# Slots declared in three dimensions, and a new order of the steps at the ends of the layers, in a fused RWKV kernel

## The chip, the cores and the metric

The kernel runs on one core of one Trainium2 chip. The metric is the device time of one execution in microseconds (us), lower is better. The kernel before was run three times: 5460.03, 5460.32 and 5466.32 us, median 5460.32.

## What is computed

The input x is (16, 192, 56, 56) float32: 16 images, 192 channels, T = 3136 positions. Three RWKV layers with different weights follow one another, then one graph convolution. Each adds its result to x:

```
for each of 3 layers:
    n = group_norm(x)                     # 32 groups of 6 channels, over all T positions
    k, v, r = Wk n, Wv n, Wr n            # 192 x 192 products at each position
    f = scan over t = 0..T-1              # decay w per channel, bonus u on the current position:
        y_t = (p + e^(u+k_t) v_t) / (q + e^(u+k_t)),   p = e^w p + e^k_t v_t,   q = e^w q + e^k_t
    b = the same scan over t = T-1..0
    h = sigmoid(r) * (f + b) / 2
    x = x + Wo (layer_norm over channels of h)
last: n = group_norm(x)
      x = x + gelu(batch_norm(conv_w [n, max of n's four neighbours at distance 2, minus n, at least 0]))
```

The group norm needs the sums over all positions of an image before the next layer can begin. That is what makes a layer have an end.

## The kernel before

All the time is spent in `fast_path`. Two images form a pair, and a tile of one pair is 128 partitions x 3 rows x columns: row 0 is 128 channels of the first image, row 2 those of the second, and row 1 the last 64 channels of both. The positions are cut into 7 chunks of L = 448 columns.

**Slots.** Chunks of x, e^k (`ek`), e^k v (`ekv`), the scans' results (`q`, `p`; `den` and `h` for the forward pass) and the sigmoid (`sg`) live in 33 slots of SBUF, which are handed out and given back in a queue (class `Slot`, L501). A slot is declared as one flat stretch of 3 * (L + 2) + 2 floats a partition. The three rows are views of it: `t` is the 448 data columns of each row, `full` has one more column at the right, `lead` one more at the left. The extra column carries two things. A scan (`scan`, L834) reads the last state of the chunk before it there, put there by `save` (L850), so that a scan of 449 columns continues it. And in the first chunk of a product it carries the mean of the group norm (`mean_column`, L753), so that PE computes the bias of a projection as one more column, which `take_bias` (L825) copies out. The semaphores between engines are placed by the framework from the regions that the instructions read and write.

**Order of the work.** Pairs run in two streams. While one stream runs its backward pass over chunks 6 to 0, the other runs its forward pass, so that a step in the middle has a backward chunk and a forward chunk (`both_a`, L1244, or `both_c`, L1336, beside the convolution). Each pass has seven chunks, shifted by one: the last forward chunk (6) is a step by itself (`forward_a`, L1386), then the first backward chunk (6) is one (`backward_alone`, L1505), then come the six double steps, of which the first is `both_a_first` (L1295) when the partner is a forward pass. The order inside a step is written out by hand: every engine takes its instructions in the order of the calls. A forward pass begins 24 times (8 pairs, 3 layers), and the convolution 8 times.

**A backward chunk** goes through: `b_gate` (product r on PE), `b_exp` (e^-r on ACT), `b_sigmoid`, `b_q`, `b_p` (scans on DVE), `b_den`, `b_num` (bonus on `ek` and `ekv`, two instructions at L860 each), inversion of `ek` on ACT (`ln` L923, `exp_minus` L926), `b_mix` (nine products on POOL, L986 to L988), `b_squares` (ACT), `b_sums` (PE), `b_rs1` (ACT, L1010), `b_rs2` (DVE, L1014), `b_rs3` (ACT, L1019 and L1020), `b_spread` (PE, L1026), `b_scale` (DVE, L1031), `b_out` (PE, the product with Wo), `b_x` (DVE, L1044) and the store, then `b_stats` (sums and squares for the next group norm, ACT, L725 and L726). `late` keeps how far a chunk has come.

**A forward chunk**: `a_values` (product v on PE; in the last chunk also `mean_column`, for r's bias), `a_q`, `a_save`, `a_den`, `a_ekv` (L898), `a_p`, `a_num`, `a_y` (POOL, L930), and `a_keys`, `a_exp` for the next chunk.

**A layer's end.** After chunk 0's `b_x`, `b_stats` runs the check of the finished layer's bounds (`require_all`, L632: one comparison at L634, one minimum at L635) and calls `begin_later` (L781), which loads the next weights and puts three parts in a list: `norm_sums` (DVE reduces the statistics at L731, PE sums the groups), `norm_var` (small DVE instructions from L738 on, `mean_column`, two on ACT) and `norm_fold` (three small DVE products and a scaling, L764 to L767; then the weights of k and v are scaled on DVE and those of r on POOL, three instructions each at L757 to L759). Each `gap()` in a step's order runs the next part of the list. `keys` runs what is left, so that `run.begun` is set before the first product of k.

Of the kernel before, what the change touches and what calls it, by code (L numbers as in the profile page):

```python
# [34 lines left out]
F32 = mybir.dt.float32  # L35
# [4 lines left out]
P = 128  # L40
# [14 lines left out]
L = 448  # L55
# [418 lines left out]
def fast_path(ctx: ExitStack, tc: tile.TileContext, flag, x, wproj, wfold, wcfold, wconst, wgroup, sums, picks, vecs, out):  # L474
# [19 lines left out]
    def name(s):  # L494
        ngen[0] += 1
        return f"{s}_{ngen[0]}"
# [4 lines left out]
    class Slot:  # L501
        def __init__(self, what):
            self.tag = free.pop(0)
            flat = keep.tile([P, 3 * (L + 2) + 2], F32, tag=self.tag, name=name(what))
            rows = lambda at: flat[:, at : at + 3 * (L + 2)].rearrange("p (j n) -> p j n", j=3)[:, :, 0 : L + 1]
            self.full, self.lead = rows(2), rows(1)
            self.t = self.full[:, :, 0:L]

        def give(self):
            free.append(self.tag)  # L510
# [14 lines left out]
    def stile(s, n=1):  # L525
        return small.tile([P, 3, n], F32, tag=s, name=name(s))
# [113 lines left out]
    def layer_params(l):  # L640
        b = NPAR * l
        dec = decays[:, 2 * l : 2 * l + 2]
        cc = const.tile([P, 2], F32, tag=f"cc{l}", name=f"fcc{l}")

        edge = const.tile([P, 3, 1], F32, tag=f"edge{l}", name=f"fedge{l}")
        grow = const.tile([P, 3, 1], F32, tag=f"grow{l}", name=f"fgrow{l}")
        w = small.tile([P, 2], F32, tag="p2", name=name("w"))
        S.activation(w, vec[:, b + DECAY_, :], AF.Exp)
        S.activation(dec, w, AF.Exp, scale=-1.0)
        for j in range(3):  # L650
            S.activation(edge[:, j, :], w[:, column(j)], AF.Exp, scale=-float(T))
            S.activation(grow[:, j, :], w[:, column(j)], AF.Exp, scale=float(T))
        G.tensor_scalar(edge, edge, -1.0, None, ALU.mult)
        uw = small.tile([P, 2], F32, tag="p2", name=name("uw"))
        V.tensor_sub(uw, vec[:, b + U_, :], w)
        require(slice(0, 2), uw, UW_MIN, ALU.is_ge)
        require(slice(0, 2), uw, UW_MAX, ALU.is_le)
        S.activation(cc, uw, AF.Exp)
        V.tensor_scalar(cc, cc, -1.0, None, ALU.add)

        wo = wos[l]
        bt = stile("lnb")
        for j in range(3):
            V.tensor_copy(bt[:, j, :], vec[:, b + BETA_, column(j)])
        ps = banks("pswob")
        project(ps, packed(wo), of(bt), 1)
        wob = const.tile([P, 2], F32, tag=f"wob{l}", name=f"fwob{l}")
        V.tensor_copy(wob[:, 0:1], ps[0][:, 0:1])
        V.tensor_copy(wob[:, 1:2], ps[1][:, 0:1])
        release(*ps)  # L670

        V.tensor_scalar(wo[:, 0:C], wo[:, 0:C], vec[:, b + GAMMA_, 0:1], None, ALU.mult)
        V.tensor_scalar(wo[:, C:WCOLS], wo[:, C:WCOLS], vec[:, b + GAMMA_, 1:2], None, ALU.mult)
        rest = cslot.t[:, 1 + l % 2, 0:C]
        V.tensor_copy(rest[:, 0:P], wo[:, C : C + P])
        V.tensor_copy(rest[LO, P:C], wo[LO, C + P : C + P + 64])
        V.tensor_copy(rest[HI, P:C], wo[HI, C + P + 64 : WCOLS])
        ps = banks("psctr")
        project(ps, packed(cmat), lambda rows, j: rest[rows, :] if j == 1 else wo[rows, 0:C], C)
        V.tensor_copy(wo[:, 0:C], ps[0][:, 0:C])  # L680
        V.tensor_copy(wo[:, C : C + P], ps[1][:, 0:P])
        V.tensor_copy(wo[LO, C + P : C + P + 64], ps[1][LO, P:C])
        V.tensor_copy(wo[HI, C + P + 64 : WCOLS], ps[1][HI, P:C])
        release(*ps)
        return dec, cc, edge, grow, wob, packed(wo)
# [21 lines left out]
    class Run:  # L707
        def __init__(self, pr, l, stats, src=None, first=None):
            self.pr, self.l, self.stats, self.src = pr, l, stats, src
            self.xa, self.xb, self.xz = {}, {}, {}  # L710
            if first is not None:
                self.xa[0] = first
            self.begun = False
            self.bias, self.ps = {}, {}
            self.ek, self.ekv, self.h, self.den, self.sg, self.rs = {}, {}, {}, {}, {}, {}
            self.m, self.ml, self.q, self.p = {}, {}, {}, {}
# [12 lines left out]
    def norm_sums(run):  # L729
        mv = small.tile([P, 2, 3], F32, tag="mv", name=name("mv"))  # L730
        V.tensor_reduce(mv, run.stats, mybir.AxisListType.X, ALU.add)  # L731
        run.ps["g"] = bank("psg")
        project_small(run.ps["g"], full_rows(gmat), lambda rows, j: mv[rows, :, j], 2)

    def norm_var(run):
        m = run.ps["g"][:, 0:6].rearrange("p (j s) -> p j s", s=2)
# [24 lines left out]
    def norm_fold(run):  # L761
        rstd, t = run.rstd, stile("gt")

        V.tensor_mul(t, rstd, rstd)  # L764
        V.tensor_mul(t, t, run.var)
        V.tensor_scalar(t, t, -0.5, 1.5, ALU.mult, ALU.add)
        V.tensor_mul(rstd, rstd, t)  # L767
        w, wr = run.weights
        if run.l == NLAYERS:
            V.tensor_sub(w[:, 0, :], w[:, 0, :], w[:, 1, :])  # L770
        fold(V, w, rstd)
        run.w = [folded(w[:, 0, :]), folded(w[:, 1, :])]
        if run.l < NLAYERS:
            fold(G, wr, rstd)
            run.w.append(folded(wr[:, 0, :]))
            run.new = new_stats()
        run.begun = True

    norms = []

    def begin_later(run):  # L781

        kv = wpool.tile([P, 2, FCOLS], F32, tag="kv", name=name("wkv"))
        if run.l == NLAYERS:
            nc.sync.dma_start(kv, wcfold)
            run.weights = kv, None
        else:
            nc.sync.dma_start(kv, wfold[run.l, :, 0:2, :])
            r = wpool.tile([P, 1, FCOLS], F32, tag="r", name=name("wr"))
            nc.sync.dma_start(r, wfold[run.l, :, 2:3, :])  # L790
            run.weights = kv, r
        load_ahead(("C" if run.l == NLAYERS else "A", run, 0))
        norms.extend((part, run) for part in (norm_sums, norm_var, norm_fold))

    def gap():
        if norms:
# [107 lines left out]
    def a_save(run, c):  # L904
        if c < NL - 1:
            save(run.den[c], AHEAD, slot_of(run.ek, c + 1, "ek"), S)
        else:
            run.last = stile("cq")
            S.activation(run.last, run.den[c].t[:, :, L - 1 : L], AF.Copy)

    def a_p(run, c, eng=G):
# [28 lines left out]

    def b_gate(run, c):
        product(run, "r", run.w[2], run.xb[c], c == NL - 1)
        if c == NL - 1:
            take_bias(run, "r", S, -1.0)

    def b_exp(run, c):
        ps, b = run.ps["r"], run.bias["r"]
        sg = run.sg[c] = Slot("sg")
        for j in ORDER:
            at = j * NL + c  # L950
            S.activation(  # L951
                sg.t[:, j, :], ps[j][:, 0:L], AF.Exp, bias=b[:, j, :], scale=-1.0, accum_out=run.chk[:, at : at + 1]
            )
            release(ps[j])
# [96 lines left out]
    def b_stats(run, c):  # L1051
        xs = run.xb.pop(c)
        chunk_stats(run.new, xs.t, c, c == 0)
        if c == 0:
            require_all(run.chk, slice(0, NCHK))
            nxt = run.follow
            nxt.stats, nxt.src = run.new, run.dst
            nxt.xa[0] = xs
            begin_later(nxt)
        else:  # L1060
            xs.give()
# [81 lines left out]
    for pr in range(npairs):  # L1143
        runs = [Run(pr, 0, new_stats() if pr < 2 else None)]
        for l in range(NLAYERS):
            runs[-1].follow = Run(pr, l + 1, None)
            runs[-1].dst = [dram.tile([P, 3, L], F32, tag=f"x{pr}_{l}_{c}", name=name("xd")) for c in range(NL)]
            runs.append(runs[-1].follow)
        chains.append(runs)
# [63 lines left out]
    def deviation(u):  # L1213
        b_rs1(*u)
        b_rs2(*u)
        b_rs3(*u)
        late[u] = 1
# [77 lines left out]
    def both_a_first(b, a, nback, nfront):  # L1295
# [16 lines left out]
        b_squares(*l, (1,))  # L1312
        if nback is not None:
            b_gate(*nback[1:])
            b_exp(*nback[1:])
        b_sums(*l)
        deviation(l)
        a_q(*a)
        keys(nfront)
        spread_and_scale(l)  # L1320
        b_squares(*b, (0,))
        a_save(*a)
        exp_keys(nfront)
        b_squares(*b, (2, 1))
        b_sums(*b)
        a_p(*a, V)
        a_den(*a)
        b_rs1(*b)
        ln(den())
# [56 lines left out]
    def forward_a(a, nback, nfront):  # L1386
# [19 lines left out]
        if l:  # L1406
# [16 lines left out]
            a_num(*a)  # L1423
            add(l)
            sum_up()
        else:
            if ahead:
                exp_keys(nfront)
# [76 lines left out]
    def backward_alone(b, nback, nfront):  # L1505
# [4 lines left out]
        b_q(*b)  # L1510
        gap()
        b_den(*b)
        gap()
        invert(b[0].ek[b[1]])
        b_sigmoid(*b)
        b_p(*b)
        gap()
        b_num(*b)
        b_mix(*b)
        for u in list(late):  # L1520
            finish(u)
        if nback is not None:
# [56 lines left out]
        assert not late and not unsummed  # L1579


    least = small.tile([P, 1], F32, tag="least", name="fleast")
    V.tensor_reduce(least, ok, mybir.AxisListType.X, ALU.min)
    ps = bank("psok")

# [92 lines left out]
```

## Time and profile before

The profiled execution took 5459.15 us, of which its span, from the first to the last instruction, is 5457.3 us.

| what | value |
|---|---|
| median of three runs | 5460.32 us |
| profiled execution, span | 5459.15 us, 5457.3 us |
| mean granted TensorE clock | 0.908 |
| DVE scans (L845) | 2016, 1070 ns each |
| DVE bonus (L860), 128x896 and 128x448 | 1151 to 1382 ns and 686 to 922 ns |
| POOL products: L986 to L988, L930 | about 1.2 us and 3.04 us each |
| POOL scaling of r's weights (L757 to L759) | 24 x (1.04 + 0.92 + 1.39) us |
| ACT's wait before the bias copies of r (L830) | 113.9 us in all |

A row of a timeline has the start in us from the span's start, the duration in us, the engine, the line of the code, the operation, the tile written and those read, the form (partitions x columns), and how many instructions are merged in it; in brackets stands the idle time of the engine ahead of it and what ended it. A row of a list of waits has the waiting engine, tile and line, then what it waited for, with the total in us, the count and the longest.

### The profile page before, as it was taken

Reading aid. Unit: us, or ns where it says so; the run is one execution under the profiler, and the core shown is the slowest. Engines: PE = TensorE matmul, PEld = TensorE weight load, DVE = VectorE, ACT = ScalarE, POOL = GpSimd, SP = SyncE. Lnnn points to the kernel's source line nnn. Section 1 sums busy time; section 2 is a strip of 40 time slices with the busy share of each in tenths; the row PEclk is TensorE's granted clock in tenths of the full one; section 3 lists DMA queues with packets and bytes.
Section 4 is the critical chain, followed back from the end, with each engine's and each line's share of the span. In section 5 each row is a group of like instructions: output and inputs, shape, how many; then the busy total and the mean of one; then the engine's idle time right before and its main releaser. Section 6 shows DMA issues by size and latency. Waiting matters only on the chain. (4 is left out here: it accounts for less than half of the span.)

```text
span 5457.3 us, 51046 instructions
## 1 busy us (share of the span) xinstructions
PE 4665.8 (85%) x15206; PEld 1502.5 (28%) x15206; DVE 5028.0 (92%) x6628; ACT 3640.3 (67%) x6891; POOL 2769.3 (51%) x2164
## 2 busy tenths in 40 slices
PE   6888988989798898888879888888888888898897
PEld 2222322223222222222222222222222222222222
DVE  6889999999999999999999999999989999999996
ACT  6776766766676676676666766666667566676673
POOL 1555555645454465554454455555535455555453
PEclk8889988989899898898989989988898999998898
DMA  5222212224343211213424212221343312122233
GB/s 147 76 78 71 83 65 75 69 92 130 95 130 88 81 66 68 73 67 110 144 76 146 66 63 76 73 73 61 114 133 92 108 56 73 61 83 78 76 101 112
DMA packets 314272, 482.43 MB, mean 88 GB/s; under 512 B 66432, under 2 KB 306688, under 8 KB 313984
## 3 DMA queue, kind: packets, MB, share of 16 engines
q1 hardware_dynamic: 312832, 477.59, 27.6%
q8 instruction: 123, 2.02, 0.2%
q10 hardware_dynamic: 1152, 1.48, 0.1%
q14 instruction: 165, 1.35, 0.1%
HBM read 324.83 MB, written 154.14 MB: 88 GB/s over the span
## 5 line engine op out<-in xcount | busy, mean ns | idle before, releaser
L845 DVE TENSOR_TENSOR_SCAN q<-fdecays,ek 128x449 f32<-128x449 f32 (+1 forms) x1008 | 1024.6, 1071 | 23.8 <-POOL p L930 13.7
L845 DVE TENSOR_TENSOR_SCAN p<-fdecays,ekv 128x449 f32<-128x449 f32 (+1 forms) x1008 | 1023.6, 1070 | 4.3 <-POOL p L930 1.6
L986 POOL TENSOR_TENSOR ekv<-ekv,ek 128x448 f32<-128x448 f32 x504 | 620.3, 1231 | 707.9 <-ACT ek L926 354.5
L930 POOL TENSOR_TENSOR p<-p,q 128x1344 f32<-128x1344 f32 x168 | 510.2, 3037 | 884.2 <-ACT q L926 469.9
L987 POOL TENSOR_TENSOR p<-p,ekv 128x448 f32<-128x448 f32 x504 | 607.5, 1205 | 39.5
L988 POOL TENSOR_TENSOR p<-p,sg 128x448 f32<-128x448 f32 x504 | 600.8, 1192 | 51.7 <-ACT ek L854 8.0
L856 POOL COPY ekv<-p 128x3 f32<-128x3 f32 x271 | 188.3, 695 | 734.8 <-DVE p L845 385.7
L1026 PE MATMUL rsb<-rs,fpicks 32*128 32x448 f32 (+1 forms) x1008 | 370.7, 649 | 166.8 <-ACT rs L1020 166.8
L880 ACT ACTIVATE ek<-k,k 128x448 f32<-128x448 f32 x504 | 293.9, 634 | 287.9 <-PE k L596 261.6
L995 ACT ACTIVATE ek<-p 128x448 f32<-128x448 f32 x504 | 283.8, 573 | 266.1 <-POOL p L988 264.6
L593 PE MATMUL ops<-p,fwo 128*128 128x448 f32 x336 | 230.5, 777 | 229.7 <-DVE p L1031 229.0
L860 DVE SCALAR_TENSOR_TENSOR q<-ek,fcc,q 128x896 f32<-128x896 f32 x336 | 348.6, 1038 | 60.4 <-ACT ek L854 52.0
L726 ACT ACTIVATE fjunk<-x 128x448 f32<-128x448 f32 x672 | 387.5, 577 | 20.4
L860 DVE SCALAR_TENSOR_TENSOR ek<-ek,fcc,q 128x896 f32<-128x896 f32 x336 | 367.2, 1093 | 8.7 <-POOL chk L936 2.8
L725 ACT ACTIVATE fjunk<-x 128x448 f32<-128x448 f32 x600 | 343.1, 572 | 12.9
L860 DVE SCALAR_TENSOR_TENSOR ekv<-ekv,fcc,p 128x896 f32<-128x896 f32 x336 | 340.7, 1014 | 7.3
L1044 DVE SCALAR_TENSOR_TENSOR x<-ops,fwob,x 128x448 f32<-128x448 f32 x504 | 314.7, 673 | 27.0 <-PE ops L602 19.6
L860 DVE SCALAR_TENSOR_TENSOR p<-ekv,fcc,p 128x896 f32<-128x896 f32 x336 | 308.6, 919 | 20.4 <-POOL ekv L856 13.6
L951 ACT ACTIVATE sg<-r,r 128x448 f32<-128x448 f32 x504 | 312.2, 625 | 19.0 <-PE r L596 13.4
L898 DVE SCALAR_TENSOR_TENSOR ekv<-v,v,ek 128x448 f32<-128x448 f32 x504 | 312.8, 676 | 0.6
L1031 DVE TENSOR_TENSOR p<-p,rsb 128x448 f32<-128x448 f32 x504 | 282.7, 614 | 31.4 <-PE rsb L1026 31.2
L923 ACT ACTIVATE ek<-ek 128x1344 f32<-128x1344 f32 x168 | 221.1, 1316 | 71.6 <-DVE ek L860 71.6
(232 smaller groups left out, 11540.2 us busy)
## 6 DMA issues: line engine op xcount, KB each, us to landing
x<-xd SPq DMA_DIRECT2D x240, 672.0 KB, 5.6
xd<-x SPq DMA_DIRECT2D x168, 672.0 KB, 3.9
x<-in_x_dram SPq DMA_DIRECT2D x320, 224.0 KB, 4.3
x<-in_x_dram SPq DMA_DIRECT2D x320, 112.0 KB, 4.3
out_dram<-ml SPq DMA_DIRECT2D x112, 224.0 KB, 2.3
ring<-xd SPq DMA_DIRECT2D x112, 168.0 KB, 3.6
wkv<-in_wfold_dram SPq DMA_DIRECT2D x24, 640.0 KB, 5.5
out_dram<-ml SPq DMA_DIRECT2D x112, 112.0 KB, 2.3
```

What stands on the lines that cost most here:

```text
L725: S.activation(junk, xt[:, j, :], AF.Identity, accum_out=stats[:, 0, j, c : c + 1])
L726: S.activation(junk, xt[:, j, :], AF.Square, accum_out=stats[:, 1, j, c : c + 1])
L845: V.tensor_tensor_scan(out, dec[:, column(j)].to_broadcast([P, L if first else L + 1]), e, 0.0, ALU.mult, ALU.add)
L860: by_channel(lambda js, i: V.scalar_tensor_tensor(dst.t[:, js, :], e.t[:, js, :], cc[:, i : i + 1], state.t[:, js, :], ALU.mult, ALU.add))
L898: V.scalar_tensor_tensor(e.t[:, j, :], ps[j][:, 0:L], b[:, j, :], run.ek[c].t[:, j, :], ALU.add, ALU.mult)
L930: G.tensor_mul(run.h[c].t, run.h[c].t, den.t)
L951: S.activation(sg.t[:, j, :], ps[j][:, 0:L], AF.Exp, bias=b[:, j, :], scale=-1.0, accum_out=run.chk[:, at : at + 1])
L986: G.tensor_mul(y.t[:, j, :], y.t[:, j, :], den.t[:, j, :])
L987: G.tensor_add(h.t[:, j, :], h.t[:, j, :], y.t[:, j, :])
L988: G.tensor_mul(h.t[:, j, :], h.t[:, j, :], sg.t[:, j, :])
L1026: PE.matmul(ps[j][:, :L], pick[rows, j, :], rs[rows, :], start=True, stop=True)
L1044: V.scalar_tensor_tensor(xj, ps[j][:, 0:L], wob[:, column(j)], xj, ALU.add, ALU.add, accum_out=run.new[:, 0, j, c : c + 1] if c == 0 else ...
```

## The change

It has six parts.

1. A slot is declared as a tile of three dimensions, 128 x 3 x (L + 4); `t`, `full` and `lead` are plain slices of it. A row is 452 floats instead of 450, 33 slots take 528 bytes more of each partition, and three small tiles share a tag with others to make room.
2. The check of the finished layer (`require_all`) moves from `b_stats` to the next layer's `norm_sums`, behind the reduction and the group product.
3. The scaling of r's weights on POOL becomes a fourth part, `norm_fold_r`, which runs in a later gap.
4. The copies of r's bias move from `b_gate` to the head of `b_exp`.
5. In `both_a_first`, `b_sums` and `b_rs1` stand ahead of `b_exp`, `a_q` ahead of `b_rs2` and `b_rs3`, and `a_p` ahead of `spread_and_scale`.
6. The gaps move: `forward_a` gains one behind `sum_up`, `backward_alone` has one behind `b_q` and one behind `b_mix` in place of three ahead of `b_den`, the inversion and `b_num`.

By the order of the calls, `norm_sums` then falls at the end of the last forward step, `norm_var` behind `b_q`, `norm_fold` behind `b_mix`, and `norm_fold_r` into the second or third double step.

```
-            flat = keep.tile([P, 3 * (L + 2) + 2], F32, tag=self.tag, name=name(what))
-            rows = lambda at: flat[:, at : at + 3 * (L + 2)].rearrange("p (j n) -> p j n", j=3)[:, :, 0 : L + 1]
-            self.full, self.lead = rows(2), rows(1)
-            self.t = self.full[:, :, 0:L]
+            rows = keep.tile([P, 3, L + 4], F32, tag=self.tag, name=name(what))
+            self.full, self.lead = rows[:, :, 2 : L + 3], rows[:, :, 1 : L + 2]
+            self.t = rows[:, :, 2 : L + 2]
...
     def norm_sums(run):
...
         project_small(run.ps["g"], full_rows(gmat), lambda rows, j: mv[rows, :, j], 2)
+        if run.before is not None:
+            require_all(run.before.chk, slice(0, NCHK))
...
     def norm_fold(run):
...
-            fold(G, wr, rstd)
-            run.w.append(folded(wr[:, 0, :]))
             run.new = new_stats()
         run.begun = True
+
+    def norm_fold_r(run):
+        if run.l < NLAYERS:
+            wr = run.weights[1]
+            fold(G, wr, run.rstd)
+            run.w.append(folded(wr[:, 0, :]))
...
-        norms.extend((part, run) for part in (norm_sums, norm_var, norm_fold))
+        norms.extend((part, run) for part in (norm_sums, norm_var, norm_fold, norm_fold_r))
...
     def b_gate(run, c):
         product(run, "r", run.w[2], run.xb[c], c == NL - 1)
+
+    def b_exp(run, c):
         if c == NL - 1:
             take_bias(run, "r", S, -1.0)
-
-    def b_exp(run, c):
...
     def b_stats(run, c):
...
         if c == 0:
-            require_all(run.chk, slice(0, NCHK))
...
     def both_a_first(b, a, nback, nfront):
...
         if nback is not None:
             b_gate(*nback[1:])
+        b_sums(*l)
+        b_rs1(*l)
+        if nback is not None:
             b_exp(*nback[1:])
-        b_sums(*l)
-        deviation(l)
         a_q(*a)
+        b_rs2(*l)
+        b_rs3(*l)
         keys(nfront)
+        a_p(*a, V)
         spread_and_scale(l)
         b_squares(*b, (0,))
         a_save(*a)
         exp_keys(nfront)
         b_squares(*b, (2, 1))
         b_sums(*b)
-        a_p(*a, V)
         a_den(*a)
...
     def forward_a(a, nback, nfront):
...
             add(l)
             sum_up()
+            gap()
         else:
...
     def backward_alone(b, nback, nfront):
...
         b_q(*b)
         gap()
         b_den(*b)
-        gap()
         invert(b[0].ek[b[1]])
         b_sigmoid(*b)
         b_p(*b)
-        gap()
         b_num(*b)
         b_mix(*b)
+        gap()
```

More of the change, by code (lines that the diff above doesn't have):

```diff
@@ L503, in __init__ @@
             self.tag = free.pop(0)
[L504 to L507, printed above, removed]
+            rows = keep.tile([P, 3, L + 4], F32, tag=self.tag, name=name(what))
+            self.full, self.lead = rows[:, :, 2 : L + 3], rows[:, :, 1 : L + 2]
+            self.t = rows[:, :, 2 : L + 2]
         def give(self):
@@ L661, in layer_params @@
         wo = wos[l]
-        bt = stile("lnb")
+        bt = stile("gt")
         for j in range(3):
@@ L712, in __init__ @@
                 self.xa[0] = first
-            self.begun = False
+            self.begun, self.before = False, None
             self.bias, self.ps = {}, {}
@@ L733, in norm_sums @@
         project_small(run.ps["g"], full_rows(gmat), lambda rows, j: mv[rows, :, j], 2)
+        if run.before is not None:
+            require_all(run.before.chk, slice(0, NCHK))
     def norm_var(run):
@@ L773, in norm_fold, with norm_fold_r @@
         if run.l < NLAYERS:
-            fold(G, wr, rstd)
-            run.w.append(folded(wr[:, 0, :]))
             run.new = new_stats()
         run.begun = True
+    def norm_fold_r(run):
+        if run.l < NLAYERS:
+            wr = run.weights[1]
+            fold(G, wr, run.rstd)
+            run.w.append(folded(wr[:, 0, :]))
     norms = []
@@ L792, in begin_later @@
         load_ahead(("C" if run.l == NLAYERS else "A", run, 0))
-        norms.extend((part, run) for part in (norm_sums, norm_var, norm_fold))
+        norms.extend((part, run) for part in (norm_sums, norm_var, norm_fold, norm_fold_r))
     def gap():
@@ L907, in a_save @@
         else:
-            run.last = stile("cq")
+            run.last = stile("cvb")
             S.activation(run.last, run.den[c].t[:, :, L - 1 : L], AF.Copy)
@@ L942, in b_gate, with b_exp @@
         product(run, "r", run.w[2], run.xb[c], c == NL - 1)
+    def b_exp(run, c):
         if c == NL - 1:
             take_bias(run, "r", S, -1.0)
-    def b_exp(run, c):
         ps, b = run.ps["r"], run.bias["r"]
@@ L1054, in b_stats @@
         if c == 0:
-            require_all(run.chk, slice(0, NCHK))
             nxt = run.follow
@@ L1146, in fast_path @@
             runs[-1].follow = Run(pr, l + 1, None)
+            runs[-1].follow.before = runs[-1]
             runs[-1].dst = [dram.tile([P, 3, L], F32, tag=f"x{pr}_{l}_{c}", name=name("xd")) for c in range(NL)]
@@ L1314, in both_a_first @@
             b_gate(*nback[1:])
+        b_sums(*l)
+        b_rs1(*l)
+        if nback is not None:
             b_exp(*nback[1:])
-        b_sums(*l)
-        deviation(l)
         a_q(*a)
+        b_rs2(*l)
+        b_rs3(*l)
         keys(nfront)
+        a_p(*a, V)
         spread_and_scale(l)
@@ L1325, in both_a_first @@
         b_sums(*b)
-        a_p(*a, V)
         a_den(*a)
@@ L1425, in forward_a @@
             sum_up()
+            gap()
         else:
@@ L1512, in backward_alone @@
         b_den(*b)
-        gap()
         invert(b[0].ek[b[1]])
@@ L1516, in backward_alone @@
         b_p(*b)
-        gap()
         b_num(*b)
         b_mix(*b)
+        gap()
         for u in list(late):
@@ L1579, in fast_path @@
         assert not late and not unsummed
-    least = small.tile([P, 1], F32, tag="least", name="fleast")
+    least = small.tile([P, 1], F32, tag="p2", name="fleast")
     V.tensor_reduce(least, ok, mybir.AxisListType.X, ALU.min)
```

## The prediction

> **What bounds the kernel now.** I read the page first: VectorE (DVE) is busy 92% of the span and close to full in nearly every slice, TensorE (PE) 85%, ScalarE (ACT) 67%, GpSimd (POOL) 51%.
>
> ```profile
> PE 4665.8 (85%) x15206; PEld 1502.5 (28%) x15206; DVE 5028.0 (92%) x6628; ACT 3640.3 (67%) x6891; POOL 2769.3 (51%) x2164
> DVE   6889999999999999999999999999989999999996
> ```
>
> So a microsecond counts when DVE loses it. DVE is idle 5457.3 - 5028.0 = 429 us. Second view, what DVE waits for (us in total, times, longest):
>
> ```profile
> DVE x L754 <- PE v L602: 54.7, 17, 4.1
> ...
> DVE rs L1014 <- ACT rs L1010: 41.7, 17, 2.8
> DVE mv L731 <- ACT fjunk L726: 35.4, 19, 20.3
> ...
> DVE nm L738 <- PE psg L602: 19.4, 17, 4.0
> ```
>
> Counts of 17 point at the 24 layer ends, not at the steady steps. At 17 of them the last forward chunk comes straight after a step that runs both directions; I call these the full ends. L754 there copies the mean into the extra column of x. PE's v product reads the other 448 columns of that x, so the wait guards nothing. SyncE shows the same kind of wait between two loads into different columns of one slot:
>
> ```profile
> SPq L817 <- DMA ring<-xd: 263.5, 56, 6.6
> ```
>
> Third view, the timeline of one full end, DVE first, then POOL (start, duration):
>
> ```profile
> 2074.78 1.92 DVE L754 COPY x<-nm 128x3 f32<-128x3 f32 x1 [2.71 <-PE v L602]
> ...
> 2092.58 1.51 DVE L634 TENSOR_TENSOR req<-chk,flimit 128x33 f32<-128x33 f32 x1
> ...
> 2106.72 2.11 DVE L860 SCALAR_TENSOR_TENSOR ekv<-ekv,fcc,p 128x896 f32<-128x896 f32 x2
> ...
> 2114.67 2.60 DVE L860 SCALAR_TENSOR_TENSOR ek<-ek,fcc,q 128x896 f32<-128x896 f32 x2
> 2117.20 3.51 DVE L860 SCALAR_TENSOR_TENSOR ekv<-ekv,fcc,p 128x896 f32<-128x896 f32 x2
> ```
>
> ```profile
> 2073.65 3.03 POOL L930 TENSOR_TENSOR p<-p,q 128x1344 f32<-128x1344 f32 x1 [4.04 <-ACT q L926]
> 2091.00 3.04 POOL L930 TENSOR_TENSOR p<-p,q 128x1344 f32<-128x1344 f32 x1 [14.32 <-DVE p L860]
> ...
> 2106.50 0.92 POOL L758 TENSOR_SCALAR wr<-wr,rstd 128x192 f32<-128x192 f32 x1
> ...
> 2114.72 2.06 POOL L988 TENSOR_TENSOR p<-p,sg 128x448 f32<-128x448 f32 x1
> ```
>
> The copy's 1.92 us (elsewhere 0.16) ends at 2076.70 with POOL's product at 2076.68, and the check's 1.51 us (its quickest is 0.19) at 2094.09 with POOL's at 2094.04. These two are busy time that is really waiting.
>
> **One rule against one row.** The Trainium skill, SBUF — State Buffer, section "SBUF: two separate sides", says that a GpSimd instruction and a VectorE one with two SBUF inputs exclude each other for the whole instruction. For POOL products the rows agree: from 2114.67 on, two bonus pairs cost 6.1 us instead of 2 x 1.84, taking turns with POOL's products. For POOL's weight scaling they do not: at 2106.72 two-input bonuses ran through L758 and L759 and cost 2.11 instead of 1.84. The change puts that scaling (1.05 + 0.92 + 1.41 = 3.4 us) next to a forward bonus. By the rule it would take up to 3.4 us at 24 ends, 81 us; by the row 0.27 x 24 = 6. I take the row, and as both old and new place pay it, nothing in the sum.
>
> **The change, part by part**, on that full end, whose old stretch runs from 2072.07 (end of the bonus before L754) to 2139.76 (next step's scan).
>
> 1. *Three-dimensional slots.* If column waits vanish, the copy runs at 2072.1 in 0.16 us, before POOL's product at 2073.65; 4.5 us go (2.71 + 1.76). What is late next: the q scan ends at 2075.25, rs2 at 2075.9, and the bonus on q meets POOL's product until 2076.68. It starts there instead of at 2080.35: 3.7 gained. After it follow L898, L1031, the p scan and bonus in unchanged order; PE's spread has moved with ACT's rs3, so b_x starts at 2087.0 instead of 2090.77. Still 3.8. The trace cannot show how a declared third dimension is tracked: 0 to 4.5 us, and I take the upper end because every such wait falls on columns of the flattened view, while x loads into separate rows of a slot (L543 to L545) wait 2 to 3 us in all. Rows 8 bytes longer cost nothing: scans of 448 and 449 elements, at different offsets, both take 1.07.
>
> 2. *Bias copies behind the squares; sums and check at the end of the forward step.* Today ACT stands 4.75 + 1.64 us at the bias copies of r ahead of c = 0's squares. Without them the squares follow b_x: the last ends near 2089.8, so the sums, which now stand ahead of b_q, wait 0.95 us (old 0.54). Queued behind that DVE wait is b_q, for which nobody waits earlier. The check now follows the sums at 2090.05, when POOL's product (2087.15 to 2090.2) is ending: 0.4 in place of 1.7. b_q runs under PE's group matmuls (behind r, done about 2093.7), so L738 waits 0.25 instead of 0.93. End of norm_var: 2094.6 against 2101.7, 7.1 gained. ACT's bias copies and exponentials then end at 2094.2, free for the inversion at 2096.4. No part moved issues a DMA; the weight and x loads stay at begin_later.
>
> 3. *e^k v bonus ahead of folding.* b_den, b_p, b_num end at 2101.3 against 2108.76: 7.5 gained. POOL's b_mix starts at 2100.4 (ek inverted at 2099.05) instead of 2108.78, no longer behind r's scaling. The price is that folding now runs during b_mix. Its three two-input products (L764, L765, L767; 0.16 each) each let one POOL product pass, 1.13 + 0.08 us less their own length: about 1.1, so 3.3. Bounds: 0 if b_mix is late, 7 x 1.1 = 7.7 if the four scalings, too, take turns; the row nearest (L757 to L759 beside POOL's scaling, 0.42, 0.58, 0.56) shows none, so 3.3. Folding ends at 2106.3: b_q starts 2.4 early. k's product now starts with the folding's end, 1.7 early; it isn't needed before a_q.
>
> 4. *both_a_first.* b_mix is over by about 2112, as b_den begins at 2112.3, so the 2.4 us of turn-taking at 2114.67 go: a_ekv ends 4.5 early, at 2118.2. Then L1014 no longer stands 2.80 us: the q scan (3.04) covers rs1, at 2120.1 because b_exp (3 x 0.61) is behind it. rs3 waits for that b_exp, the p scan covers it, and L1031 waits 0.2 or so instead of 0.34. New: the p copy (L856) and the bonus on q now lie beside the next b_mix, 0.9 + 1.3; b_x may wait 0.2. Next step's scan at 2134.6 against 2139.76: 5.2 gained. ACT's rs1 and inversion are 3.9 early, with slack.
>
> 5. *r's weights deferred* to a later gap: POOL stands 4 to 7 us before L930 at each step, which hides 3.4; without that cover 3.4. *Tags*: startup, nothing.
>
> Sum: 13 full ends with both_a_first, 13 x 5.2 = 68; 4 full ends into the convolution, where part 4 is missing but L754 (m) waits 2.2 for the same b_mix, 4 x 4 = 16; both_a_first after 4 other ends, L1014's 0.85 (once 2.8) and L1031, 4. At the tail the chain that ended last has three pairs of ring loads in series (5358.76, 5404.43, 5423.21); together they save about 1.4, 2.2 and 2.9: 6. In all 94. The profiled execution took 5459.15 us (span 5457.3), 1.2 under the median of 5460.32; I take 94 off the median: 5366.
>
> **The rivals.** (a) *Slots change no wait.* For: the hardware pattern is the same. Against: waits sit on flattened columns only. L754 stays, part 1's 3.8 and the tail are lost: 17 x 1.4 + 4 = 28, 5432. (b) *Slower: folding starves.* Place: backward_alone. If DVE gets no turn until b_mix's nine products (10.9 us) are through, folding ends at 2113.5, b_q is 4.7 late, part 4 returns 2.8: -1.9 x 17 = -32, with 10 from elsewhere 5482. It decides once folding stalls over 3.3 + 5.2 = 8.5 us. Against: at 2114.67 DVE gets every second turn. (c) *No collisions at folding and in the first step,* POOL late or DVE first: 5.2 + 3.3 = 8.5 x 17 + 10 = 155, 5305.
>
> **Chances.** Main 0.64 (own range 5330 to 5405), (a) 0.15, (c) 0.13, (b) 0.08. Range 5305 to 5440: it takes in (a) and the edge of (c). A measurement here tells 0.2% (11 us) from no change. Slower is (b), 0.08; same is (a)'s low end, 0.04; faster 0.88.
>
> **What would show it.** L754 without a PE wait and at 0.16; L817 not waiting; L634 near 0.2; L1014's wait under 5 us in total; L764 to L767 above 1 us at the full ends; L860 ek and ekv of both_a_first at 1.84. Wrong if L754 still waits, or folding lasts over 6 us.

## The result, and the profile after

The changed kernel takes 5382.74 us (median of four runs, 5381.18 to 5385.39), the kernel before 5460.17 in the same session: a ratio of 0.9856 (95% interval 0.9839 to 0.9873), 77.4 us less. The prediction said 94. The profiled execution has a span of 5379.3 us. Its page first:

```profile
PE 4618.0 (86%) x15206; PEld 1484.1 (28%) x15206; DVE 5004.0 (93%) x6628; ACT 3634.0 (68%) x6891; POOL 2784.1 (52%) x2164
```

DVE is still the busiest engine, at 93% of the span. It has lost 24 us of busy time, and its idle time fell from 429 to 375. What DVE waits for now (us in total, times, longest):

```profile
DVE mv L730 <- ACT fjunk L725: 69.5, 25, 20.2
...
DVE gt L765 <- ACT rstd L748: 29.4, 8, 4.8
...
DVE rs L1019 <- ACT rs L1015: 23.4, 17, 1.8
...
DVE nm L739 <- PE psg L601: 17.2, 19, 2.7
```

The mean copy's wait for PE (54.7 us) is gone from the list, and so is the wait between the two ring loads. But the sums (`mv`) wait twice as long as before and at 25 places instead of 19, and the wait for `rstd` at the folding's first product (`gt`) has grown from 0.7 to 29.4. The full end that the prediction worked through now looks like this (timeline, DVE):

```profile
2044.81 0.16 DVE L755 COPY x<-nm 128x3 f32<-128x3 f32 x1
...
2063.77 0.18 DVE L633 TENSOR_TENSOR req<-chk,flimit 128x33 f32<-128x33 f32 x1
...
2075.29 1.11 DVE L765 TENSOR_TENSOR gt<-rstd 128x3 f32<-128x3 f32 x1
...
2076.63 0.99 DVE L767 TENSOR_SCALAR gt<-gt 128x3 f32<-128x3 f32 x1
...
2077.85 1.18 DVE L758 TENSOR_SCALAR wkv<-wkv,rstd 128x384 f32<-128x384 f32 x1
2078.95 1.28 DVE L759 TENSOR_SCALAR wkv<-wkv,rstd 128x384 f32<-128x384 f32 x1
2080.15 1.35 DVE L760 TENSOR_SCALAR wkv<-wkv,rstd 128x512 f32<-128x512 f32 x1
...
2088.99 1.74 DVE L865 SCALAR_TENSOR_TENSOR ekv<-ekv,fcc,p 128x896 f32<-128x896 f32 x2
...
2097.53 0.63 DVE L1019 TENSOR_TENSOR rs<-st,rs 64x448 f32<-64x448 f32 x1 [1.80 <-ACT rs L1015]
```

Copy and check are as short as foretold, and the bonus pairs of `both_a_first` no longer take turns with POOL. But folding lasts from 2075.29 to 2081.43, 6.14 us: over the 6 us at which the prediction called itself wrong. The end of L765 (2076.40) falls on that of POOL's first product, the end of L767 (2077.62) on that of the second. POOL:

```profile
2074.93 1.46 POOL L991 TENSOR_TENSOR ekv<-ekv,ek 128x448 f32<-128x448 f32 x1
2076.46 1.13 POOL L992 TENSOR_TENSOR p<-p,ekv 128x448 f32<-128x448 f32 x1
```

And L1019 (L1014 before) still waits 1.80, 23.4 in all, where under 5 was foretold. So the total was near, and at least one step was not.

### The profile page after: what moved, and what is told of

The parts are those of the page before. It is cut to its first block, busy times and chain, and to the rows that moved or that the text cites. A ratio compares the mean times of both kernels' runs of the same rounds, so it can differ in the third digit from the quotient of the medians.

```text
span 5379.3 us, 50906 instructions
## 1 busy us (share of the span) xinstructions
PE 4618.0 (86%) x15206; PEld 1484.1 (28%) x15206; DVE 5004.0 (93%) x6628; ACT 3634.0 (68%) x6891; POOL 2784.1 (52%) x2164
## 5 line engine op out<-in xcount | busy, mean ns | idle before, releaser
L850 DVE TENSOR_TENSOR_SCAN q<-fdecays,ek 128x449 f32<-128x449 f32 (+1 forms) x1008 | 1024.3, 1070 | 23.8 <-POOL p L935 15.6
L861 POOL COPY ekv<-p 128x3 f32<-128x3 f32 x271 | 215.1, 794 | 726.9 <-DVE p L850 564.5
L865 DVE SCALAR_TENSOR_TENSOR q<-ek,fcc,q 128x896 f32<-128x896 f32 x336 | 388.4, 1196 | 35.8 <-ACT ek L859 29.9
L1031 PE MATMUL rsb<-rs,fpicks 32*128 32x448 f32 (+1 forms) x1008 | 349.2, 609 | 74.1 <-ACT rs L1025 74.1
L1049 DVE SCALAR_TENSOR_TENSOR x<-ops,fwob,x 128x448 f32<-128x448 f32 x504 | 317.0, 673 | 33.9 <-PE ops L601 23.4
L865 DVE SCALAR_TENSOR_TENSOR ek<-ek,fcc,q 128x896 f32<-128x896 f32 x336 | 343.6, 1063 | 3.1 <-POOL chk L941 3.1
L865 DVE SCALAR_TENSOR_TENSOR p<-ekv,fcc,p 128x896 f32<-128x896 f32 x336 | 297.7, 927 | 16.3 <-POOL ekv L861 15.7
L1036 DVE TENSOR_TENSOR p<-p,rsb 128x448 f32<-128x448 f32 x504 | 281.3, 613 | 32.2 <-PE rsb L1031 32.2
L865 DVE SCALAR_TENSOR_TENSOR ekv<-ekv,fcc,p 128x896 f32<-128x896 f32 x336 | 297.7, 927 | 1.2
```

The lines of the kernel that those rows point to most:

```text
L850: V.tensor_tensor_scan(out, dec[:, column(j)].to_broadcast([P, L if first else L + 1]), e, 0.0, ALU.mult, ALU.add)
L865: by_channel(lambda js, i: V.scalar_tensor_tensor(dst.t[:, js, :], e.t[:, js, :], cc[:, i : i + 1], state.t[:, js, :], ALU.mult, ALU.add))
L1031: PE.matmul(ps[j][:, :L], pick[rows, j, :], rs[rows, :], start=True, stop=True)
L1049: V.scalar_tensor_tensor(xj, ps[j][:, 0:L], wob[:, column(j)], xj, ALU.add, ALU.add, accum_out=run.new[:, 0, j, c : c + 1] if c == 0 else ...
```

## The experiments

The theory (A) after these rows: the slots carry more than the prediction gave them, and the new order gives part of it back. The rival (B) was the prediction's own view, in which the order of the layer ends carries much of the gain. Four runs first.

**slots_only** is the kernel before with the new `Slot` class and tags, and the old order everywhere:

```
-            flat = keep.tile([P, 3 * (L + 2) + 2], F32, ...)
+            rows = keep.tile([P, 3, L + 4], F32, ...)
```

> The kernel before with three-dimensional slots and the renamed small tiles, the old order of steps everywhere. Theory A (the slots carry most of the gain: the 17 column waits of about 3.8 us at the mean copy, and bonus halves that no longer wait for each other): 5400 us, 55 to 65 under the kernel before; the copy of the mean shows no PE wait, and the second bonus instruction of a pair starts before the first has ended. Rival B (the new order of the layer ends carries most of the gain, the slots free waits that the next instruction gives back): 5440 us, 20 under.

Measured: 5327.41 us, ratio 0.9758 (0.9745 to 0.9771). This is 132 us under the kernel before and 55 us *under the whole change*. Theory A had the sign, and was itself too low by half.

**order_only** is the changed kernel with the old flat slot in place of the new one, so it has all of the new order and nothing of the slots.

> The changed kernel with the flat slots of before. Theory A: the reordering gains about 28 us at the full ends, and gives some 25 back at the six places after a convolution where DVE now waits for the statistics: 5450 us, near the kernel before; the mean copy waits for PE's v product again. Rival B: 5405 us.

Measured: 5487.29 us, 1.0049 (1.0035 to 1.0063): slower than the kernel before by 28 us. Rival B falls, and theory A's 5450 is missed too: the order alone is not neutral, it costs. The change is a large gain from the slots and a loss from the order, and what has to be found is which part of the order loses.

**gap_last** keeps the gap that was added to `forward_a` to the last chunk:

```
             sum_up()
-            gap()
+            if a[1] == NL - 1:
+                gap()
```

> The changed kernel with the new gap of the forward step kept to the last chunk of a pass (chunk 6), so that the six first chunks after a convolution do their scan before the sums, as in the kernel before. Theory A (that gap makes DVE wait for ACT's squares, 5.6 us, and for rstd, 4.8 us, and some 4 to 6 us of it reach the end each time): 5355 us, 20 to 35 under the changed kernel, and the rstd waits at the folding's first product (29.4 us in all) are gone. Rival B (the wait is only moved within the step): 5380 us, no difference.

Measured: 5346.29 us, 0.9794 (0.9780 to 0.9807), 36 us under the changed kernel, as theory A had it. The branch that got the gap also runs in the first forward chunk after a convolution, at six places. What happens there in the changed kernel:

```profile
1608.71 0.20 DVE L730 TENSOR_REDUCE mv<-stats 128x6 f32<-128x42 f32 x1 [5.64 <-ACT fjunk L725]
...
1623.68 0.16 DVE L765 TENSOR_TENSOR gt<-rstd 128x3 f32<-128x3 f32 x1 [4.82 <-ACT rstd L748]
```

DVE stands 5.64 us for ACT's squares, with the forward scans queued behind, and then 4.82 for `rstd`. In gap_last the `mv` waits number 19 again (32.2 us in all), and the `rstd` waits sum to 0.5.

**flat_keys** was meant to bring back the flat slot for e^k and e^k v alone. It declares them flat, but 3 * (L + 4) = 1356 floats long, and cuts the rows out after rearranging the whole tile.

> The changed kernel, but the slots of e^k and e^k v alone are flat and rearranged as before; x and all others stay three-dimensional. Theory A (two bonus instructions on rows 0, 2 and on row 1 of one slot wait for each other when the slot is flat, 0.12 us per pair, 672 pairs, of which steps that POOL's product limits give most back): 15 to 30 us slower than the changed kernel, 5405 us, and a pair beside no POOL work at 1.84 instead of 1.73. If all of the 0.12 counted: 5463. Rival B (all absorbed elsewhere): 5383 us.

Measured: 5386.75 us, 0.9866 (0.9851 to 0.9881), the time of the changed kernel. But the run doesn't test the theory: in its trace the second bonus instruction of a pair still starts 84 ns before the first has ended, as in the changed kernel, where with the old slot it starts 35 ns after. So this flat tile had none of the old spacing, and "flat" as such isn't the cause. The next two runs take the old slot of 1352 floats exactly.

**x_old and rest_old** split the slots' gain. Both are slots_only with two kinds of slot. In x_old, x and the ring have the old one; in rest_old, all others have it:

```
+            if what in ("x", "ring"):        # rest_old: not in
+                flat = keep.tile([P, 3 * (L + 2) + 2], F32, ...)
```

> The slots-only kernel (5327), but x and the ring keep the old flat slot of 1352 floats; all other slots are three-dimensional. Theory A (the column waits of x are most of what the slots give: 17 full ends of 4.6 us each by the trace of the slots-only kernel, 78 us, and some of the ring loads): 5406 us, the mean copy waits for PE's v product again, and bonus pairs stay at 1.73. Theory B (bonus halves that overlap, 0.12 us on 672 pairs, carry most): 5350 us.

> The slots-only kernel, but x and the ring alone are three-dimensional; e^k, e^k v, q, p, sigmoid and the others keep the old flat slot of 1352 floats. Theory A: 5380 us, 50 over the slots-only kernel, with bonus pairs at 1.85 again and the mean copy at 0.16 without a PE wait. Theory B: 5408 us, 81 over it.

Measured: x_old 5407.14 us, 0.9892 (0.9877 to 0.9907); rest_old 5370.93 us, 0.9826 (0.9813 to 0.9839). Against slots_only the old slots of x cost 80 us, those of the others 44; together 124 of the 132. Theory A's split holds. In x_old the mean copy waits again:

```profile
DVE x L759 <- PE v L607: 62.5, 17, 4.2
```

The other part shows in the second instruction of each bonus pair, row 1 after rows 0 and 2. The last column is its idle time, first in the list of groups of rest_old and then in that of slots_only:

```profile
L865 DVE SCALAR_TENSOR_TENSOR ek<-ek,fcc,q 128x448 f32<-128x448 f32 x168 | 157.1, 935 | 6.0
```

```profile
L859 DVE SCALAR_TENSOR_TENSOR ek<-ek,fcc,q 128x448 f32<-128x448 f32 x168 | 163.2, 971 | 0.0
```

6.0 us on 168 instructions are 36 ns of standing each. Undisturbed pairs take 1.86 us in rest_old and 1.73 in slots_only, since the second instruction there starts before the first has ended. 672 pairs at 0.12 to 0.13 would be 81 to 87 us; 44 reached the end. 11 us of the rest are given back in the bonus on q, 128x896, whose 168 instructions take 1539 ns on average in rest_old and 1607 in slots_only; where the others go was not followed.

**slots_first and slots_ends** take the order apart, each on top of slots_only. slots_first has the new `both_a_first` alone. slots_ends has the new layer end alone: `gap` in the last forward chunk (as in gap_last), check behind the sums, folding behind `b_mix`, r's scaling later.

> The slots-only kernel with the new order of both_a_first and nothing else of the reordering. Theory A (this part is good: by the traces the first double step gains about 2.1 us at 13 to 19 ends): 5290 to 5300 us. Rival (what the first double step gains is given back, as DVE then runs into POOL's products in the steady steps after it): 5325 to 5345 us.

> The slots-only kernel with the new layer end and nothing else: sums and check at the end of the last forward chunk (chunk 6 alone), folding after b_mix, r's scaling in a later gap; both_a_first and the bias copies as before. Theory A (this part costs: DVE waits for the squares before the backward scan, 1.6 us, and folding takes turns with b_mix, 2.8 to 4 us): 5327 plus 13 to 17 times 3, 5365 to 5380 us. Rival (the prediction: norm_var ends earlier and the bonus on e^k v comes ahead of folding, at least 2 us a full end gained): 5290 us.

Measured: slots_first 5315.60 us, 0.9724 (0.9710 to 0.9737), 12 less than slots_only, between the two expectations. slots_ends 5421.21, 0.9917 (0.9903 to 0.9930): 94 *more* than slots_only, and more than theory A had. Its waits say why:

```profile
DVE mv L730 <- ACT fjunk L725: 117.2, 19, 16.3
DVE rs L1019 <- ACT rs L1015: 61.8, 21, 4.8
```

At a full end of it the sums, now ahead of the backward scan, wait 5.89 us, because ACT's bias copies of r still stand ahead of the squares. So early sums need the later bias copies. first_back, below, differs from slots_ends by these copies alone and takes 67 us less, where the same move is worth 30 with the old layer end.

**slots_first_bias** puts r's bias copies behind the squares, with the old layer end. **check_behind** moves the check behind the sums as well, but leaves both in the backward step after its scan of q, and puts r's scaling behind `b_mix`; k's and v's folding stays ahead of the bonus on e^k v.

```
     def b_gate(run, c):                      # slots_first_bias
         product(run, "r", ...)
-        if c == NL - 1:
-            take_bias(run, "r", S, -1.0)
     def b_exp(run, c):
+        if c == NL - 1:
+            take_bias(run, "r", S, -1.0)
```

```
         b_p(*b)                              # check_behind, backward_alone
         gap()
         b_num(*b)
         b_mix(*b)
+        gap()
```

> The kernel with three-dimensional slots and the new both_a_first (5316), and in addition r's bias copies moved behind the squares; layer end otherwise as before. Theory A (ACT's bias copies stand ahead of three squares for which the sums wait 1.4 us at each full end): 17 x 1.5 = 25 us less, 5290 us. Rival (the exponentials behind the copies are late in their place, and b_mix with them): 5310 to 5325 us.

> As slots_first_bias, and the check of the bounds moved behind the sums (still in the backward step, after its scan of q), r's scaling in a later gap behind b_mix; the folding of k's and v's weights stays ahead of the bonus on e^k v. Theory A (the check's 1.3 us of taking turns with POOL's product becomes 0.2 to 0.4, and the bonus on e^k v loses its 0.38 beside r's scaling): 17 x 1.4 = 24 us less than slots_first_bias, 5266 us. Rival (the scaling behind b_mix holds up POOL's product of the next forward chunk): 5290 us or more.

Measured: slots_first_bias 5285.11 us, 0.9676 (0.9662 to 0.9689), 30 less than slots_first; check_behind 5275.79 us, 0.9656 (0.9642 to 0.9669), another 9 less. The second is the fastest kernel of this study, 107 us under the changed one. It got 9 of the 24 us expected, and 5276 lies between theory and rival. A full end of it, DVE:

```profile
2209.39 0.17 DVE L730 TENSOR_REDUCE mv<-stats 128x6 f32<-128x42 f32 x1
2209.48 0.18 DVE L633 TENSOR_TENSOR req<-chk,flimit 128x33 f32<-128x33 f32 x1
...
2211.75 0.16 DVE L739 TENSOR_SCALAR nm<-psg 128x3 f32<-128x3 f32 x1 [0.20 <-PE psg L601]
```

Sums and check wait for nothing there: the scan of q (3.05 us) ahead of them covers ACT's last squares.

**first_back and fold_ahead** start from gap_last. first_back undoes the new `both_a_first`. fold_ahead has the folding of k and v ahead of the bonus on e^k v:

```
         b_p(*b)                              # fold_ahead, backward_alone
+        gap()
         b_num(*b)
```

Since each gap runs the next part of the list, this one line moves two parts, not one as the expectation below says: folding goes into the new gap, and r's scaling into the gap behind `b_mix`, which in gap_last has the folding. In gap_last r's scaling runs in the second double step, 88 us behind the mean copy; in fold_ahead, 43 us behind it. POOL, first gap_last, then fold_ahead:

```profile
2312.12 1.20 POOL L758 TENSOR_SCALAR wr<-wr,rstd 128x192 f32<-128x192 f32 x1
```

```profile
2240.80 0.77 POOL L758 TENSOR_SCALAR wr<-wr,rstd 128x192 f32<-128x192 f32 x1
```

> gap_last (5346) with the old order of both_a_first; sums and check in the last forward chunk, folding behind b_mix, bias copies behind the squares. Theory A (the late folding makes k's product, the r product and the statistics of chunk 6 late, and only the new both_a_first covers that wait, about 3 us at 13 ends): 5346 + 40 = 5386 us. Rival (both_a_first is worth the same as on the slots-only kernel, 12 us): 5358 us.

> gap_last (5346) with the folding of k's and v's weights ahead of the bonus on e^k v again; r's scaling stays in the gap behind b_mix. Theory A (beside b_mix the folding takes 6.2 us instead of 2.25, and nothing is won by the earlier bonus on e^k v): 5346 - 17 x 1.7 to 3.9, 5280 to 5317 us. Rival (the prediction's part 3: the bonus comes later again, b_mix with it, and two bonus pairs of the first double step take turns with it again): 5360 us or more.

Measured: first_back 5354.39 us, 0.9803 (0.9789 to 0.9816): 8 more than gap_last. The new `both_a_first` is worth about as much as on slots_only (12), and theory A, which saw it as the cover of the late folding (40), fails here: the waits of L1019 do grow by 42 us (65.5 against 23.8), but the bonus on q takes 20 less, and the waits before `b_x` are 15 less. fold_ahead 5295.66 us, 0.9697 (0.9684 to 0.9710): 51 *less* than gap_last, within theory A. Folding behind the bonus, the prediction's part 3, with r's scaling pushed into a later step, is the dearest step of the change.

The ladder; the sums are the differences of the medians:

| kernel | us | part added | its worth |
|---|---|---|---|
| before | 5460 | | |
| slots_only | 5327 | slots | -132 |
| slots_first | 5316 | `both_a_first` | -12 |
| slots_first_bias | 5285 | bias copies behind squares | -30 |
| check_behind | 5276 | check behind sums, r's scaling behind `b_mix` | -9 |
| fold_ahead | 5296 | sums and check ahead of the backward scan, norm_var ahead of the bonus on e^k | +20 |
| gap_last | 5346 | folding behind the bonus, r's scaling into the second double step | +51 |
| after | 5383 | the same gap after a convolution | +36 |

The rungs were measured in several sessions, in which the kernel before took 5459 to 5465 us. Taken as ratios to it, slots_first is worth 18 instead of 12, first_back differs from gap_last by 5 instead of 8, and x_old and rest_old cost 74 and 37 instead of 80 and 44. So the smallest rungs have a sign rather than a size; those of 20 us and more move by 3 at most. A rung's worth also depends on those below it: the whole order costs 28 us on the old slots and 55 on the new.

## Why the prediction was right in its total and wrong in its terms

**Part 1, the slots: the copy's term was right, and another was missing.** The copy starts without a wait and takes 0.16, and the ring loads no longer wait. The copies as groups by shape, in the kernel before and in slots_only:

```profile
L754 DVE COPY x<-nm 128x3 f32<-128x3 f32 x56 | 39.5, 705 | 55.4 <-PE v L602 54.7 <-DMA x<-in_x_dram 0.4 <-DMA xd<-x 0.3
```

```profile
L753 DVE COPY x<-nm 128x3 f32<-128x3 f32 x56 | 9.0, 161 | 0.0
```

They lose 30.5 us of length and 55.4 of waiting. At the 17 full ends the bonus on q behind them, which then meets POOL's product, takes 23 us more in all (1.15 us each before, up to 3.63 in slots_only). 63 us stay, 3.7 a full end, where the prediction had 3.8. The tail, from the last such copy to the end, is 5.2 us shorter (95.6 to 90.4), where it had 6. What it did not see is that the same slots also kept apart instructions of one engine on different rows: it took every such wait to fall on columns. rest_old puts the other slots at 44 us. The list of waits doesn't show these. They are 36 ns long, and show only in the groups kept apart by shape, where 168 second instructions have 6.0 us of idle time and nobody is named. About 20 us of the 132 have no place in this account. And that the third dimension as such frees the accesses isn't shown: in flat_keys e^k and e^k v lack it, and their pairs are not kept apart.

**Part 2, bias copies, sums and check: two gains and a loss.** The copies' place is worth 30 us, 1.8 a full end. The check is at 0.18, and `mv` waits 0.80 where 0.95 was said. But L739 waits 0.94 instead of 0.25, and the step that failed is the choice of place: the wait before `b_q` was taken as a price for ending norm_var 7.1 us earlier. Nothing on DVE was short of norm_var; DVE's own queue is the path, and both stands reach it. The rung from check_behind to fold_ahead shows their size; the waits of fold_ahead, then of check_behind:

```profile
DVE mv L730 <- ACT fjunk L725: 36.5, 19, 20.2
...
DVE nm L739 <- PE psg L601: 20.2, 20, 3.7
```

```profile
DVE mv L730 <- ACT fjunk L725: 21.5, 2, 20.3
...
DVE nm L739 <- PE psg L601: 11.1, 18, 3.8
```

That is 24 us more of standing. Measured: 20.

**Part 3, the bonus ahead of folding: wrong.** The failed step is the sentence that k's product "isn't needed before a_q", and with it the wait of L1014 that was to go. Compare the same stretch, from the mean copy to the next step's scan: 64.99 us in gap_last (2224.15 to 2289.14), 59.90 in fold_ahead (2197.40 to 2257.30). DVE, first gap_last, then fold_ahead:

```profile
2266.44 1.72 DVE L865 SCALAR_TENSOR_TENSOR ek<-ek,fcc,q 128x896 f32<-128x896 f32 x2
...
2276.55 0.63 DVE L1019 TENSOR_TENSOR rs<-st,rs 64x448 f32<-64x448 f32 x1 [1.74 <-ACT rs L1015]
...
2281.41 1.69 DVE L1036 TENSOR_TENSOR p<-p,rsb 128x448 f32<-128x448 f32 x3 [0.87 <-PE rsb L1031]
```

```profile
2224.36 0.13 DVE L765 TENSOR_TENSOR gt<-rstd 128x3 f32<-128x3 f32 x1
...
2225.14 0.42 DVE L758 TENSOR_SCALAR wkv<-wkv,rstd 128x384 f32<-128x384 f32 x1
2225.48 0.42 DVE L759 TENSOR_SCALAR wkv<-wkv,rstd 128x384 f32<-128x384 f32 x1
2225.81 0.48 DVE L760 TENSOR_SCALAR wkv<-wkv,rstd 128x512 f32<-128x512 f32 x1
...
2233.78 2.60 DVE L865 SCALAR_TENSOR_TENSOR ek<-ek,fcc,q 128x896 f32<-128x896 f32 x2
2236.31 3.51 DVE L865 SCALAR_TENSOR_TENSOR ekv<-ekv,fcc,p 128x896 f32<-128x896 f32 x2
...
2244.84 0.63 DVE L1019 TENSOR_TENSOR rs<-st,rs 64x448 f32<-64x448 f32 x1
```

Folding takes 1.84 us in fold_ahead and 6.14 in gap_last: +4.3, where the prediction had +3.3. In fold_ahead the two bonus pairs take turns with `b_mix` again, 5.96 instead of 3.30: -2.7, as it said (2.4). The rest, it missed: in gap_last L1019, L1036 and L1049 wait 1.74 + 0.87 + 0.18, together +2.8. In the prediction the q scan "covers rs1", and 0.4 is left for the other two. In fold_ahead L1019 follows without a wait. These three are 4.4 of the 5.1 us. Why the wait is there shows on PE, first gap_last, then fold_ahead:

```profile
2258.38 1.84 PE L592 MATMUL k<-x,wkv 128*128 128x449 f32 x2 [6.73 <-DVE wkv L758]
...
2274.21 0.57 PE L1007 MATMUL st<-p,fsums 128*32 128x448 f32 x2
```

```profile
2225.82 0.99 PE L592 MATMUL k<-x,wkv 128*128 128x449 f32 x2 [2.56 <-DVE wkv L758]
...
2239.32 0.57 PE L1007 MATMUL st<-p,fsums 128*32 128x448 f32 x2
```

PE takes its products in order: k, v, r, and then the statistics `st` for which L1019 waits. k starts 34.2 us after the mean copy in gap_last, 28.4 in fold_ahead. Everything behind k is late with it, though k's result itself isn't needed: `st` starts 50.1 us after the copy in gap_last, 41.9 in fold_ahead. 5.8 us of the difference are k's later start. The other 2.3 are k's product itself, which PE begins at half clock after its long stand (the last section has the rows): from k to `st` it needs 15.8 us in gap_last, 13.5 in fold_ahead and in the kernel before. That is why `st` is late against the kernel before, too, though k starts earlier: measured from the end of the bonus ahead of the copy, k starts at 34.2 us (35.1 in the kernel before; 1.7 early was foretold, 0.9 came), `st` at 50.0 (48.6).

This end is one of the dearest. Taken to the next step's L1019, the stretch is 1.0 to 5.1 us longer in gap_last at the 13 ends with `both_a_first`, 3.4 on average. The five steps behind it, in the first of which gap_last scales r's weights, add 0.8 more; how much of that is r's scaling isn't settled. At the 4 ends into the convolution gap_last is 1.4 shorter. 13 x 4.2 - 4 x 1.4 = 49 of the 51 us. So most of the 51 us is the folding and what it holds up.

The size of folding itself, too, was a wrong choice between bounds. Of the three two-input products for which the prediction gave 1.1 us each, only the first pays (1.11 in the rows of the changed kernel), the other two take 0.16. It took the four scalings as not blocked, from rows in which they ran beside POOL's *scaling*. Beside POOL's *products* they take 0.99, 1.18, 1.28 and 1.35 us instead of 0.17, 0.42, 0.42 and 0.48. Where nothing disturbs it, a scaling pays 0.06 us for 128 more columns, 0.47 ns each, against 1.04 ns in a bonus ((1151 - 686) / 448, the quickest means in the table of before). The Trainium skill, SBUF — State Buffer, section "SBUF: two separate sides", counts not only two-input VectorE instructions among those that exclude GpSimd, but also those in a two-port mode; a doubled rate is what its page "VectorE: DVE Perf Modes", section "Mode 2×_2P — use both read ports for one tensor", describes; that the scalings ran in this mode no run here shows. The prediction used one of the two kinds. With both, it would have taken its own upper bound, 7.7 us, close to the 8.5 from which its rival (b) decides; measured are 4.3, and the waits on PE beside them.

**Part 4, `both_a_first`: right.** The prediction's 5.2 us an end is a running total of all parts; this step's own share is its growth from 4.5 (`a_ekv`) to 5.2, 0.7 at 13 ends, with 4 us at other ends: 13 in all. Measured: 12 on slots_only, 8 on gap_last. Its terms are there in slots_first: of 46.5 us of idle time before L1014's instruction 41 go, and the bonus on q and the copy of p, now beside `b_mix`, take 22 and 3 more.

**Part 5, r's scaling hidden:** no run prices it alone. Behind `b_mix`, and with the check, it is worth -9; with it in a later double step, as in the change, the steps around it are 0.8 us an end longer than in fold_ahead.

**Not foreseen:** the gap in `forward_a` fires at six ends after a convolution, +36. The prediction followed one kind of end and never asked where else the edited branch runs.

So the prediction's 94 is not a right sum, and that it came within 17 us of the measured 77 is luck: a gain that was missed and losses that were missed nearly cancel. It had 71 for the slots (17 x 3.8 and the tail's 6) and 23 for all the rest. The slots gave 132; `both_a_first`, bias copies and check gave 51; early sums, late folding and the six other ends took back 107. Rival (b) had the right place. In its own terms, with DVE getting no turn until `b_mix` is through, it didn't happen: in gap_last folding ends at 2260.6, `b_mix` at 2265.1. What late folding cost is 3.0 us a full end on average (51 / 17), below the 8.5 from which the rival would have decided by itself.

## What to carry to other kernels

On an in-order engine "not needed until later" is not free: before moving a step back, list what stands behind its consumer in that consumer's queue. When a change gains, run its parts alone all the same; here one of seven was worth more than the whole, and the kernel without three of them is 107 us faster than the change. An added step in a shared branch has to be followed at every place where the branch runs, not at the one that it was meant for.

## What the runs showed of the hardware

- The two DVE instructions of a bonus pair, on different rows of one slot, overlap by 77 to 85 ns with the new slot (slots_only) and stand 35 ns apart with the old one (rest_old): 0.12 us for each pair of 1.73.
- DVE's scalings of 384 to 512 columns take turns with POOL's products (0.42 to 1.18 us), and even a 128x3 product or scaling can lose 0.8 to 1 us so (0.13 to 1.11, 0.17 to 0.99), while the 128x3 product between them takes its 0.16.
- After standing 6.73 us PE came back at half clock. In the table of stretches of gap_last, PEclk (third number from the end) is 0.50 in the 4 us in which k's first products ran, 0.93 in the 8 us after; the first pair took 1.84 us instead of 0.99. After 2.56 us of standing, in fold_ahead, it stayed at 1.00. The length of one stand doesn't decide it alone: 20 us earlier in fold_ahead, after stands of 2.12 and 1.05 us close together, it was 0.50 from 2206.40 to 2209.60.

```profile
2258.00:2262.00 4.00, 3.62 (x6) 1.49 (x8) 4.00 (x5) 0.00 (x0) 3.84 (x4) 0.50 0.01 4
2262.00:2270.00 8.00, 8.00 (x25) 2.42 (x24) 8.00 (x13) 4.90 (x11) 3.98 (x4) 0.93 0.00 1
```

- What of the old slot made the waits isn't settled by these runs: a flat slot of 1352 floats, rows 450 apart, had them (x_old, rest_old); a flat one of 1356, rows 452 apart and cut otherwise, did not for e^k and e^k v (flat_keys).
